# LSTM gates as seven half-size products for two groups at a time, and layer 2's output through DRAM

## The chip, the cores and the metric

The kernel runs on one core of a Trainium2 chip. The metric is the device time of one execution in microseconds (us), taken as the median of several runs. TensorE (PE) multiplies matrices into PSUM; VectorE (DVE), ScalarE (ACT) and GpSimd (POOL) do the elementwise work; SyncE (SP) issues the DMAs.

## What is computed

Four graph layers, each followed by a residual sum and a layernorm, on x of 128 batches x 64 nodes x 256 features, all in float32. The first three are a graph attention, an attention over 512 edges, and a graph convolution with a two-layer network and batch norm. The fourth is the one that the change is about: two graph convolutions, then LSTMs of 256 hidden units over windows of 1, 2, 3 and 4 nodes, one after the other, each of which writes its last output back into h.

```python
def step(carry, x_t):
    h, c = carry
    g = x_t @ Wih.T + h @ Whh.T + bias
    i, f, gg, o = jnp.split(g, 4, axis=-1)
    c = jax.nn.sigmoid(f) * c + jax.nn.sigmoid(i) * jnp.tanh(gg)
    h = jax.nn.sigmoid(o) * jnp.tanh(c)
    return ((h, c), None)
...
h = jax.nn.relu(jnp.einsum('ts,bsh->bth', adj, x @ Wg0 + bg0))
h = jax.nn.relu(jnp.einsum('ts,bsh->bth', adj, h @ Wg1 + bg1))
for p in range(1, MAX_SKIP + 1):
    nw = Tv // p
    wins = h[:, :nw * p, :].reshape(Bv * nw, p, Hd)
    last = _lstm_last(Wih[p - 1], Whh[p - 1], bih[p - 1], bhh[p - 1], wins)
    idx = jnp.arange(nw) * p + (p - 1)
    h = h.at[:, idx, :].set(last.reshape(Bv, nw, Hd))
```

## The kernel before

The 128 batches are worked in 16 blocks of 512 tokens (`q`) in layers 0 to 2. Layer 2's result stays in SBUF in the tile `A`, 1024 float32 in each of 128 partitions for each block (`leave`, L791). Layer 3 takes it in eight groups of 16 batches (`g`), each of two halves (a half is one block).

`gcn(g, half, ...)` is layer 3 for a half, cut in pieces by `yield`: the batch norm's scale on ACT (L890), a transpose (on TensorE for group 0 at L897, through DVE and a round trip over DRAM, `turned`, for the later ones), the residual sum and layernorm (`norm`; bn_stats on DVE at L92, a power on GpSimd at L83, the scaling on GpSimd at L97), the products with the adjacency (`neighbours`, L878) and with Wg0 and Wg1 (L933, L945), and the write of `H` (L956 on DVE, L957 on ACT).

`lstm(g)` runs the windows p = 1 to 4 on one group. The hidden size of 256 is two halves of 128 (`j` for outputs, `k` for inputs). A unit of work is one half j of one step: for each of the gates i, f, g, o, two matmuls with `wih` (L994) and, after the first step, two with `whh` (L1000) accumulate in one of five PSUM banks, over 512 columns for p=1 and p=2, 336 for p=3 and 256 for p=4. ACT takes each bank through sigmoid or tanh (L1006); DVE and GpSimd form the cell (L1009 to L1011, or L1013 in the first step); ACT its tanh (L1014); DVE the output (L1021, L1023). A float32 matmul in the program is two instructions in the profile.

After every unit, pieces of the next group's `gcn` and of `final` (the last residual sum, layernorm and store of a group, for one of four node residues s) are put in by a written list of units (`AT`, `side`). They are ordered behind the last instruction on ACT, DVE and GpSimd. SP issues nearly all loads and stores in program order. The weights of all four p are loaded once: `wih` and `whh` of 1 MB each for p=2, 3, 4.

The prologue of layer 3 runs the two halves of group 0 in turn before the first LSTM unit, and the last `final` (with `pieces=2`) follows the last unit.

Of the kernel before, what the change touches and what calls it, by code (L numbers as in the profile page):

```python
# [41 lines left out]
def kernel(ctx: ExitStack, tc: tile.TileContext, i, out):  # L42
# [9 lines left out]
    A = main.tile([P, NQ, 2 * QT], F32, name="A")  # L52
# [32 lines left out]
    def layernorm(dst, src, n, engine):  # L85

        st = small.tile([P, n, 6], F32, name="ln_st", bufs=6)
        mv = small.tile([P, n, 2], F32, name="ln_mv", bufs=6)
        both = small.tile([P, 2, n], F32, name="ln_rs", bufs=6)
        rs, ng = both[:, 0, :], both[:, 1, :]  # L90
        for r in range(n):
            nc.vector.bn_stats(st[:, r, :], src[:, r, :])  # L92
            nc.vector.bn_aggr(mv[:, r, :], st[:, r, :])
        rsqrt(rs, mv[:, :, 1], n)
        nc.vector.tensor_scalar_mul(ng, mv[:, :, 0], -1.0)  # L95
        for r in range(n):
            engine.tensor_scalar(dst[:, r, :], src[:, r, :], ng[:, r:r + 1], rs[:, r:r + 1],  # L97
                                 op0=OP.add, op1=OP.mult)
# [13 lines left out]
    with ExitStack() as two:  # L112
        wa = two.enter_context(tc.tile_pool(name="wa", bufs=1))
# [12 lines left out]
        def load_x(q):  # L126
            xin[q] = xp.tile([P, PQ, D], F32, name="xin")
            nc.sync.dma_start(xin[q], x_view[q])
            if q:

                rows = i["x"][q * QT:(q + 1) * QT, :].rearrange("(j t) (k i f) -> i k t j f", t=32, k=KD, f=32)
                for n in range(4):
                    for k in range(KD):
                        to = A[n * 32:(n + 1) * 32, q, k * QT:(k + 1) * QT]
                        nc.sync.dma_start(to.rearrange("t (j f) -> t j f", f=32), rows[n, k])

        class su:

            free = NQ * 2 * QT

            @classmethod
            def tile(cls, shape, dtype, name):
# [4 lines left out]
                t = A.rearrange("p q c -> p (q c)")[:shape[0], cls.free:cls.free + size]  # L147
# [60 lines left out]
        def token_major(q):  # L208

            return A[:, q, :].rearrange("p (c d) -> p c d", c=PQ)  # L210

# [3 lines left out]
        def l0_a(q):  # L215
            L0[q] = {"x": xin.pop(q)}
            if q:

                L0[q]["xT"] = work.tile([P, KD, QT], F32, name="tT", bufs=1)
                nc.vector.transpose(L0[q]["xT"].rearrange("p k t -> p (k t)"), A[:, q, :])  # L220
# [199 lines left out]
        def v_c(q, one=True):  # L420
# [14 lines left out]
            dst = A[:, q, :].rearrange("p (b s n) -> p s b n", b=KD * PQ, s=2)  # L435
# [270 lines left out]
        def hidden(q, m):  # L706
            return Z[q][:, m, :] if m < 2 else A[:, q, (m - 2) * QT:(m - 1) * QT]

# [7 lines left out]
        def up(q, m):  # L716
            p_ = pbank()
            for k in range(KD):
                nc.tensor.matmul(p_, w1[:, k, m * P:(m + 1) * P], A[:, q, k * QT:(k + 1) * QT],  # L719
# [31 lines left out]
        wih, whh = {}, {}  # L751
        wih[1] = wd.tile([P, KD, 3 * D], F32, name="wih1")
        v1 = i["WihT"][0].rearrange("(k p) c -> p k c", p=P)
        nc.sync.dma_start(wih[1][:, :, :D], v1[:, :, :D])
        nc.sync.dma_start(wih[1][:, :, D:], v1[:, :, 2 * D:])
        wih[2] = weights(wd, "wih2", i["WihT"][1])
        whh[2] = weights(wd, "whh2", i["WhhT"][1])
# [30 lines left out]
        def leave(q, m, p_):  # L788

            dst = A[:, q, :].rearrange("p (n m t) -> p n m t", n=PQ, m=M2)[:, :, m, :]  # L790
            nc.vector.tensor_scalar_add(dst, p_.rearrange("p (n t) -> p n t", n=PQ), b2[:, m:m + 1])  # L791

# [33 lines left out]
    work = ctx.enter_context(tc.tile_pool(name="work3", bufs=2, reuse_waits="tile"))  # L826
    ps = ctx.enter_context(tc.tile_pool(name="ps3", bufs=1, space=PSUM, reuse_waits="tile"))
    for p in (3, 4):
        wih[p] = weights(we, f"wih{p}", i["WihT"][p - 1])
        whh[p] = weights(we, f"whh{p}", i["WhhT"][p - 1])  # L830
    out_view = out.rearrange("(b t) d -> b t d", t=N)
    HT = QT // 2
    GB = 16
    ST = 5
    TC = P // GB
    NG = NB // GB
    assert GB * N == 2 * QT

    def gbank(shape):
        return ps.tile([P] + shape, F32, name="g", bufs=3)  # L840

    def lbank(shape):
        return ps.tile([P] + shape, F32, name="l", bufs=5)


    rb = we.tile([P, KD, P], F32, name="rb")
# [7 lines left out]
    Hs, lasts = {}, {}  # L854
# [27 lines left out]
    def gcn(g, half, bank, name):  # L882

        q = g * 2 + half
        def fetch(a):
            x = work.tile([P, 2, D], F32, name="x2r", bufs=4)
            nc.sync.dma_start(x.rearrange("p c d -> p (c d)"), x2_dram[q][:, a * 2 * D:(a + 1) * 2 * D])
            z = A[:, q, a * QT:(a + 1) * QT].rearrange("p (c m t) -> p c m t", c=2, m=KD)
# [3 lines left out]
            if g:  # L892
                return x, turned(z.rearrange("p c m t -> p (c m) t"))
# [4 lines left out]
            return x, xt  # L898

        def norm(a, x, xt):  # L900
            xv = x.rearrange("p c (m i f) -> p c m i f", m=KD, f=32) if g else x
            nc.vector.tensor_add(xv, xt, xv)
            x3 = A[:, q, a * QT:(a + 1) * QT].rearrange("p (c d) -> p c d", c=2)
# [5 lines left out]
        if g:  # L909
# [4 lines left out]
            for a in range(2):  # L914
                norm(a, *came[a])
                yield
        else:
            for a in range(2):
                norm(a, *fetch(a))
                yield  # L920

        x3 = A[:, q, :].rearrange("p (c d) -> p c d", c=PQ)
        p_ = neighbours(bank, lambda c, f: x3[:, c, f:f + 64])
        hT = work.tile([P, KD, QT], F32, name=name, bufs=2)
# [4 lines left out]
        hN = work.tile([P, KD, QT], F32, name=name, bufs=2)  # L929
# [23 lines left out]
        if g not in Hs:  # L953
            Hs[g] = work.tile([P, KD, N, GB], F32, name="H")
        dst = Hs[g].rearrange("p k t (h c s) -> p h s k c t", h=2, s=2)[:, half]
# [4 lines left out]
    GCN_STEPS = 8  # L960

    def lstm(g):

        H = Hs[g]
        for p in range(1, SKIP + 1):
            nw = N // p
            nww = min(nw, QT // GB)
            for w0 in range(0, nw, nww):

                Hw = H[:, :, w0 * p:(w0 + nww) * p, :].rearrange("p k (w s) b -> p k w s b", s=p)  # L970
                cell = work.tile([P, KD, nww, GB], F32, name="cell", bufs=1)
                hid = None
                for s in range(p):
                    last = s == p - 1

                    over = last and p < SKIP
                    if over:
                        new = None
                    elif last:

                        new = work.tile([P, 2, KD, P], F32, name="hd", bufs=3)
                    else:
                        new = work.tile([P, KD, nww, GB], F32, name="hid")
                    ends = []
                    for j in range(KD):
                        gates = {}
                        names = ("i", "f", "g", "o") if s else ("i", "g", "o")
                        for n in names:
                            gates[n] = ps.tile([P, nww, GB], F32, name="l", bufs=5)
                        for n in names:  # L990
                            m = 2 * "ifgo".index(n) + j
                            mw = m - 2 if p == 1 and m > 1 else m
                            for k in range(KD):
                                nc.tensor.matmul(gates[n], wih[p][:, k, mw * P:(mw + 1) * P], Hw[:, k, :, s, :],  # L994
                                                 start=k == 0, stop=not s and k == KD - 1)
                        if s:
                            for n in names:
                                m = 2 * "ifgo".index(n) + j
                                for k in range(KD):
                                    nc.tensor.matmul(gates[n], whh[p][:, k, m * P:(m + 1) * P], hid[:, k],  # L1000
                                                     start=False, stop=k == KD - 1)
                        act = {}
# [135 lines left out]
```

## Time and profile before

| | us |
|---|---|
| median of 3 runs (2138.45 to 2139.91) | 2138.93 |
| the profiled execution | 2138.25 |
| its span, first to last instruction | 2136.4 |
| end of layer 2's last matmuls | 771.5 |
| first LSTM matmul | 807.4 |
| last LSTM matmul | 2126 |

The granted TensorE clock was 0.987 on average. HBM traffic was 67.45 MB read and 44.04 MB written, at a mean DMA load of 53 GB/s. In the profile, a group's "busy" is the time that its instructions cover together, its "mean" the duration of one from issue to end; matmuls overlap, so the mean is longer than the distance between two of them. "Idle before" is the time that the engine stood still ahead of the group, with the engine and line that ended most of it. In rows in order of time, the first number is the start, the second the time covered, and xN says how many instructions are merged.

### The profile page before, as it was taken

How to read it: one execution, taken by the hardware profiler on the slowest of the kernel's cores; microseconds unless marked ns; L12 is line 12 of the kernel's file. 1: busy time of each engine (PE TensorE's matmuls, PEld its weight loads, DVE VectorE, ACT ScalarE, POOL GpSimd, SP SyncE). 2: the span in 40 equal slices, each digit the busy share in tenths (PEclk: the TensorE clock that was granted, in tenths of full speed). 3: DMA queues.
4: the chain of work that ended last, by engine and by line, in shares of the span. 5: the costliest groups of instructions: out<-in, count | busy, mean ns of one | idle time of the engine just before them, and what ended most of it. 6: DMA issues, size and time to landing. Idle time of an engine off the chain costs nothing.

```text
span 2136.4 us, 29441 instructions
## 1 busy us (share of the span) xinstructions
PE 2060.7 (96%) x11343; PEld 1330.1 (62%) x11343; DVE 885.9 (41%) x2069; ACT 932.1 (44%) x1795; POOL 430.1 (20%) x569
## 2 busy tenths in 40 slices
PE   5999999998999989999999999999999999999998
PEld 4666767665544444585576576577467468468467
DVE  7456566654444343333234334324324324323213
ACT  2776666664339014334234334334334334333333
POOL 1134334332210010121112112113103103102012
PEclk8999999998999989999999999999999999999999
DMA  5244532322240021012112102103103102101001
GB/s 144 63 69 73 85 61 53 52 43 43 43 118 29 0 89 60 21 54 66 40 46 74 40 29 90 40 11 99 50 6 104 50 1 89 50 1 60 20 1 60
DMA packets 232636, 113.41 MB, mean 53 GB/s; under 512 B 150192, under 2 KB 215728, under 8 KB 232240
## 3 DMA queue, kind: packets, MB, share of 16 engines
q1 hardware_dynamic: 230640, 109.57, 20.2%
q8 instruction: 89, 1.46, 0.3%
q0 software_dynamic: 1024, 1.05, 0.2%
q10 hardware_dynamic: 832, 0.92, 0.1%
q14 instruction: 51, 0.42, 0.1%
HBM read 67.45 MB, written 44.04 MB: 52 GB/s over the span
## 4 chain that ended last, share of the span: by engine, by line
PE 86%; DVE 6%; ACT 4%; issue 2%; POOL 1%; DMA 1%; SPq 0%; POOLq 0%; DVEq 0%; ACTq 0%
PE l L994 36%; PE l L1000 20%; PE pz L784 5%; PE pz L719 5%; PE e L323 3%; PE g L933 2%; PE g L945 2%; PE m L295 2%; PE m L230 2%; PE z L332 2%; PE m L298 2%; PE g L878 1%; PE m L413 1%; PE m L270 1%; ACT u L334 1%
## 5 line engine op out<-in xcount | busy, mean ns | idle before, releaser
L994 PE MATMUL l<-H,wih 128*128 128x256 f32 (+2 forms) x2496 | 787.5, 470 | 1.8 <-ACT H L957 1.2
L994 PEld LDWEIGHTS l<-H,wih 128*128 128x128 f32 x2496 | 471.4, 190 | 286.2 <-issue 185.6
L1000 PE MATMUL l<-hid,whh 128*128 128x256 f32 (+2 forms) x1536 | 435.9, 437 | 0.0
L1000 PEld LDWEIGHTS l<-hid,whh 128*128 128x128 f32 x1536 | 291.8, 190 | 128.4 <-issue 61.2
L1006 ACT ACTIVATE gate_i<-l,bias 128x256 f32<-128x256 f32 (+2 forms) x176 | 100.3, 570 | 441.9 <-PE l L1000 374.2
L1010 POOL TENSOR_TENSOR cell<-gate_f,cell 128x256 f32<-128x256 f32 (+2 forms) x96 | 85.0, 885 | 726.0 <-ACT gate_f L1006 726.0
L1009 DVE TENSOR_TENSOR gate_i<-gate_i,gate_g 128x256 f32<-128x256 f32 (+2 forms) x96 | 49.6, 517 | 415.1 <-ACT gate_g L1006 415.0
L83 POOL TENSOR_TENSOR ln_rs<-ln_rs,mhalf 128x2 f32<-128x2 f32 (+2 forms) x97 | 82.0, 846 | 571.6 <-DVE ln_rs L95 570.7
L334 ACT ACTIVATE u<-z 128x1024 f32<-128x1024 f32 x128 | 130.3, 1025 | 63.3 <-PE z L332 62.3
L1006 ACT ACTIVATE gate_g<-l,bias 128x256 f32<-128x256 f32 (+2 forms) x176 | 100.3, 570 | 107.9 <-PE l L994 59.5
L1014 ACT ACTIVATE gate_g<-cell 128x256 f32<-128x256 f32 (+2 forms) x176 | 90.0, 511 | 86.9 <-DVE cell L1013 45.0
L1013 DVE TENSOR_TENSOR cell<-gate_i,gate_g 128x512 f32<-128x512 f32 (+2 forms) x80 | 48.2, 602 | 186.5 <-ACT gate_g L1006 186.4
L1006 ACT ACTIVATE gate_o<-l,bias 128x256 f32<-128x256 f32 (+2 forms) x176 | 99.3, 564 | 59.9 <-PE l L1000 54.0
L719 PE MATMUL pz<-A,w 128*128 128x512 f32 x256 | 113.1, 595 | 0.0
L332 PE MATMUL z<-gath_r,qs 128*128 128x512 f32 x256 | 100.4, 480 | 0.7 <-ACT u L334 0.4
L306 DVE TENSOR_TENSOR qs<-m,qs 64x256 fp32r<-64x256 f32 x128 | 54.0, 422 | 107.0 <-ACT qs L305 104.8
L719 PEld LDWEIGHTS pz<-A,w 128*128 128x128 f32 x256 | 47.9, 190 | 55.3 <-issue 53.3
L295 PE MATMUL m<-wq,tT 128*128 128x260 f32 x256 | 71.8, 403 | 7.8 <-ACT yT L403 5.4
L1006 ACT ACTIVATE gate_f<-l,bias 128x256 f32<-128x256 f32 (+2 forms) x96 | 51.1, 532 | 59.6 <-PE l L1000 59.1
L1023 DVE TENSOR_TENSOR hid<-gate_o,gate_g 128x256 f32<-128x256 f32 (+2 forms) x96 | 47.4, 493 | 61.2 <-ACT gate_o L1006 35.1
L721 DVE BATCH_NORM_STATS2 st<-pz 128x6 f32<-128x512 f32 x64 | 44.4, 697 | 59.5 <-PE pz L719 59.4
L1023 DVE TENSOR_TENSOR H<-gate_o,gate_g 128x512 f32<-128x512 f32 (+1 forms) x64 | 41.3, 645 | 66.6 <-PE l L994 46.1
(242 smaller groups left out, 2525.2 us busy)
## 6 DMA issues: line engine op xcount, KB each, us to landing
way<-st SPq DMA_DIRECT2D x59, 256.0 KB
st<-way SPq DMA_DIRECT2D x236, 64.0 KB
xin<-in_x SPq DMA_DIRECT2D x16, 512.0 KB
ld<-table SPq DMA_DIRECT2D x16, 512.0 KB
x_dram<-y SPq DMA_DIRECT2D x16, 512.0 KB
x2r<-x_dram SPq DMA_DIRECT2D x32, 256.0 KB
x_dram<-A SPq DMA_DIRECT2D x64, 128.0 KB
x3r<-x_dram SPq DMA_DIRECT2D x64, 128.0 KB
```

Source lines behind the costliest of these rows:

```text
L83: nc.gpsimd.tensor_tensor(dst, dst, mhalf[:, :n], OP.pow)
L295: nc.tensor.matmul(pq, xT[:, k, c * P:(c + 1) * P], wq[:, k, :], start=k == 0, stop=k == KD - 1)
L332: nc.tensor.matmul(z[:, k, :], L1[q]["qs"][c][:, s, k * P:(k + 1) * P], gath_r, start=True, stop=True)
L334: nc.scalar.activation(u, z, AF.Relu)
L719: nc.tensor.matmul(p_, w1[:, k, m * P:(m + 1) * P], A[:, q, k * QT:(k + 1) * QT], start=k == 0, stop=k == KD - 1)
L784: nc.tensor.matmul(p_, w2[:, k, m * P:(m + 1) * P], hidden(q, k), start=k == 0, stop=k == M1 - 1)
L994: nc.tensor.matmul(gates[n], wih[p][:, k, mw * P:(mw + 1) * P], Hw[:, k, :, s, :], start=k == 0, stop=not s and k == KD - 1)
L1000: nc.tensor.matmul(gates[n], whh[p][:, k, m * P:(m + 1) * P], hid[:, k], start=False, stop=k == KD - 1)
L1006: nc.scalar.activation(act[n], gates[n], AF.Tanh if n == "g" else AF.Sigmoid, bias=bias[:, p - 1, m:m + 1])
L1010: nc.gpsimd.tensor_tensor(cell[:, j], act["f"], cell[:, j], OP.mult)
L1014: nc.scalar.activation(act["g"], cell[:, j], AF.Tanh)
L1023: nc.vector.tensor_mul(Hw[:, jj, :, s, :] if over else new[:, jj], o, t)
```

## The change

Three things change.

1. **Two groups at a time, seven products.** `lstm(pair)` treats two groups (n = 0, 1) together. In every step after the first of p = 2 to 4, a gate's 2 x 2 blocks of weights (output half, input half) times the 2 x 2 blocks of inputs (input half, group) are formed with seven products of 128 x 128 blocks instead of eight, for the input with `wih` and for the hidden state with `whh`, both accumulated in one bank. For this the sums of weight blocks (`Weights.sums`, four GpSimd adds for each source), of input blocks (`input_sums`, four GpSimd adds a step) and of hidden blocks (`hidden_sums`, two on DVE and two on GpSimd) are formed beforehand, and the seven products are put together by two ACT copies, five DVE adds and two GpSimd adds a gate (`Gate.use`). The gates run one after the other, f, g, i, o. Each gate's activations, cell work and tanh are issued within the next gate (`prev.act`, `prev.after`, `prev.tanh`). At a step's end the first four products' input parts of the next step's gate f are issued ahead of the outputs (`nxt.part`). p=2 runs in two runs of 16 windows, so that its matmuls have 256 columns. First steps (`plain`) keep their plain products, at 256 columns for p=2.
2. **An order for all engines.** `given` issues every piece behind the latest instruction of each of PE, DVE, ACT and GpSimd. Pieces of `gcn`, `final` and the weights' `prepare` go to written units of a pair (48 of them, of kinds "at", "gap" and "wait").
3. **Layer 2's output through DRAM.** `A` is split: blocks 0 to 3 stay in `A0`; blocks 4 to 15 are written to `z_dram` as they are done, and are read back into `A0` by `gcn`. The space gives room to weights with their sums; the weights of p = 2, 3 and 4 are loaded anew for each pair, into two alternating buffers. Halves 2 and 3 are transposed on TensorE too, and the prologue runs parts of four halves. The PSUM banks go from five "l" and three "g" to six and two.

```diff
-    A = main.tile([P, NQ, 2 * QT], F32, name="A")
+    A0 = main.tile([P, NA, 2 * QT], F32, name="A0")
+    z_dram = [dram.tile([P, 2 * QT], F32, name=f"z_dram{q}") for q in range(NQ)]
...
+            if q >= NA and m == M2 - 1:
+                nc.sync.dma_start(z_dram[q], Aq(q))
...
+            for dst, a, b, op in ((S3, a11, a21, sub), (S1, a21, a22, add), (S2, S1, a11, sub), (S4, a12, S2, sub)):
+                nc.gpsimd.tensor_tensor(dst, a, b, op)
...
+            def sums_of(dst, b11, b12, b21, b22, fast, slow, between=None):
+                fast.tensor_tensor(dst[:, 0], b12, b11, OP.subtract)
+                if between:
+                    between()
+                fast.tensor_tensor(dst[:, 1], b22, dst[:, 0], OP.subtract)
+                slow.tensor_tensor(dst[:, 2], b22, b12, OP.subtract)
+                slow.tensor_tensor(dst[:, 3], b21, dst[:, 1], OP.subtract)
...
+                def product(self, j):
+                    for src in range(2):
+                        given(self.part, j, src)
+                    given(self.use, j)
+
+                def use(self, j):
+                    b, k, t = self.banks[j], self.kept, self.t
+                    if j in (1, 5):
+                        nc.scalar.activation(self.keep(j), b, AF.Copy)
+                    elif j == 2:
+                        nc.vector.tensor_add(t[0][:, 0], b, k[1])
+                    elif j == 6:
+                        nc.vector.tensor_add(t[0][:, 1], b, k[1])
+                    elif j == 7:
+                        nc.vector.tensor_add(self.keep(7), b, t[0][:, 1])
+                        nc.gpsimd.tensor_tensor(t[1][:, 1], k[7], k[5], OP.add)
+                        nc.gpsimd.tensor_tensor(t[0][:, 1], t[0][:, 1], k[5], OP.add)
+                    elif j == 4:
+                        nc.vector.tensor_add(t[1][:, 0], b, k[7])
+                    else:
+                        nc.vector.tensor_add(t[0][:, 1], b, t[0][:, 1])
...
+                        names = "fgio"
+                        for at, n in enumerate(names):
+                            G = nxt or Gate(n, r, s, tiles)
+                            nxt = None
+                            G.product(1)
+                            G.product(5)
+                            if prev:
+                                prev.act(1)
+                                prev.act(0)
+                                prev.after(1)
+                            G.product(2)
+                            if prev:
+                                prev.after(0)
+                                prev.tanh(1)
+                            G.product(6)
+                            if n == "o":
+                                G.act(0, 0)
+                            if prev:
+                                prev.tanh(0)
+                            G.product(7)
+                            if at == 1:
+                                given(input_sums, r, s + 1)
+                            if at < 3:
+                                G.product(4)
+                                G.product(3)
+                                yield "at", unit
...
+                        o.product(4)
+                        given(output, r, s, 0, o.tiles["o"], o.tiles["g"], (0,))
+                        o.act(1)
+                        o.product(3)
+                        o.act(0, 1)
+                    if not last:
+                        tiles = {}
+                        nxt = Gate("f", r, s + 1, tiles)
+                        for j in (1, 5, 2, 6):
+                            given(nxt.part, j, 0)
+                    elif p < SKIP:
+                        yield "wait", unit + 1
+                    if s:
+                        given(output, r, s, 0, o.tiles["o"], o.tiles["g"], (1,))
+                        given(hidden_sums, s, lambda: output(r, s, 1, o.tiles["o"], o.tiles["g"], (0, 1)))
...
+                put(k + 1, final(g, SKIP - 1), n, n + 2)
+        if k < NP - 1:
+            put(k, prepare(weights_of[k + 1, 2]), 34, 41, 43)
+            for n, keys in enumerate([
+                    [0, 2, 3, 5, 6, 10, 15, 17, WAIT(22), GAP(22), 24],
+                    [2, 5, 6, 8, 9, 19, GAP(25), 26, GAP(29), 30, 32],
+                    [6, 8, 9, 12, 13, 27, WAIT(33), GAP(33), GAP(36), 37, 39],
+                    [9, 11, 12, 15, 16, 38, GAP(40), 41, GAP(44), 45, 47]]):
+                put(k, gcn((k + 1) * 2 + n // 2, n % 2, gbank, "hT"), *keys)
```

In a pair, units 0 to 7 are p=1, 8 to 21 p=2, 22 to 32 p=3 and 33 to 47 p=4; within p=4, step 0 is units 33 to 35, and then each step has a unit after f, g and i and one at its end.

## The prediction

> **What bounds the kernel now.** I read the page first (busy shares, slices, chain), then the busy time of three stretches, then TensorE's groups by shape, then single steps in order of time. The page:
>
> ```profile
> PE 2060.7 (96%) x11343; PEld 1330.1 (62%) x11343; DVE 885.9 (41%) x2069; ACT 932.1 (44%) x1795; POOL 430.1 (20%) x569
> ...
> PE   5999999998999989999999999999999999999998
> ...
> PE 86%; DVE 6%; ACT 4%; issue 2%; POOL 1%; DMA 1%; SPq 0%; POOLq 0%; DVEq 0%; ACTq 0%
> ```
>
> TensorE is the only engine near its span, and the chain that ended last runs on it. The stretches (columns: PE, PEld, DVE, ACT, POOL busy, clock, DMA) show the start of layer 3, its LSTM and the tail:
>
> ```profile
> 771.50:807.40 35.90, 26.53 (x323) 19.12 (x322) 19.61 (x51) 7.76 (x12) 7.62 (x13) 0.76 0.40 133
> 807.40:2126.00 1318.60, 1317.36 (x6160) 856.05 (x6161) 443.61 (x1002) 499.09 (x911) 226.51 (x321) 1.00 0.15 47
> 2126.00:2137.00 11.00, 0.95 (x6) 0.41 (x4) 3.14 (x13) 0.89 (x2) 2.19 (x4) 0.67 0.09 24
> ```
>
> In the LSTM, TensorE idles 1.2 us of 1318.6. A matmul taken out there is worth its full pitch, and a microsecond of new waiting costs a microsecond. The matmuls by shape:
>
> ```profile
> L994 PE MATMUL l<-H,wih 128*128 128x512 f32 x832 | 363.6, 593 | 1.8 <-ACT H L957 1.2 <-ACT gate_g L1014 0.5
> L994 PE MATMUL l<-H,wih 128*128 128x256 f32 x960 | 217.2, 380 | 0.0
> L994 PE MATMUL l<-H,wih 128*128 128x336 f32 x704 | 206.8, 448 | 0.0
> L1000 PE MATMUL l<-hid,whh 128*128 128x256 f32 x768 | 173.6, 379 | 0.0
> L1000 PE MATMUL l<-hid,whh 128*128 128x336 f32 x512 | 149.9, 446 | 0.0
> L1000 PE MATMUL l<-hid,whh 128*128 128x512 f32 x256 | 112.5, 592 | 0.0
> ```
>
> The mean is a latency; the pitch is what counts. Starts in order of time: 16 of 256 columns take 3.455 us (1949.51 to 1952.96), 16 of 336 take 4.52, 16 of 512 take 6.866. So 0.216, 0.2825 and 0.429 us for each instruction, and each product in the program is two of them. The pitch is linear in columns, so halving a matmul's width costs nothing.
>
> **What the Trainium skill says.** "TensorE: Matmul & The Clock Gate", Part 1: after an idle window of about 3.4 us the array runs at half clock until about 3.4 us of work have passed. The trace agrees; the first four products after the gaps at the start took twice the time of the next:
>
> ```profile
> 788.66 3.43 PE L933 MATMUL g<-hT,wg 128*128 128x512 f32 x4
> ...
> 791.93 1.88 PE L933 MATMUL l<-hid,wg 128*128 128x512 f32 x4
> ```
>
> "SBUF — State Buffer", Who interferes with whom: a VectorE instruction with two SBUF inputs and a GpSimd instruction that reads SBUF exclude each other; one with a single SBUF input is free. The trace has mild cases, 0.58 instead of 0.42 us:
>
> ```profile
> 2107.51 0.72 POOL L1010 TENSOR_TENSOR cell<-gate_f,cell 128x256 f32<-128x256 f32 x1
> 2108.18 0.94 POOL L1035 COPY hd<-H 128x256 f32<-128x256 f32 x2
> 2108.27 0.58 DVE L1011 TENSOR_TENSOR cell<-cell,gate_i 128x256 f32<-128x256 f32 x1 [2.48 <-POOL cell L1010]
> ...
> 2121.97 0.42 DVE L1011 TENSOR_TENSOR cell<-cell,gate_i 128x256 f32<-128x256 f32 x1 [2.48 <-POOL cell L1010]
> ```
>
> **The change part by part.**
>
> *Matmuls.* Later steps go from 8 to 7 products for each gate, source and pair. p=2: 512 instructions of 512 columns (219.7 us) become 4 pairs x 2 runs x 4 gates x 7 x 2 sources x 2 = 896 of 256 (193.5): -26.2. p=3: 1024 to 896 of 336: -36.2. p=4: 1536 to 1344 of 256: -41.5. p=2's first step, 192 of 512 to 384 of 256: +0.5. Sum -103.4. Halves 2 and 3 are now transposed on TensorE: 16 more at about 0.21 (0.85 for four at L897): +3.4.
>
> Each still hides its weight load, 0.19 under 0.216 (PEld rows of a step: 3.43 for 16 beside 3.62).
>
> *The additions beside them.* A p=4 product with both sources takes 0.86 us, a gate 6.05. A gate adds two ACT copies (0.39, L232's 258-column row), five VectorE adds (0.43) and two GpSimd adds (0.72). At 2.2 us of DVE in 6.05 they are hidden in gates f, g and i. PSUM has six banks, so TensorE may run 5 us ahead. Not so in gate o, where i's finish also lies. From o's start U: ACT copies product 5 at 1.9 to 2.3, then i's two sigmoids (0.63 each) to 3.55; DVE mul and add for m=1 (0.69 each) 2.95 to 4.33, use of product 2 to 4.76, m=0's mul and add to 6.14, uses of 6 and 7 to 7.0; GpSimd's two adds to 8.5; DVE's use of product 3 to 8.96; ACT to 9.48; hid to 9.93; first hidden sum 10.35. TensorE finishes o at 6.05, runs four prefetched products and one more part (5 x 0.432) to 8.21 and then wants that sum. It waits 2.2 us, and 0.25 for the second half of hid: 2.45. The same chain with p=3 (DVE 0.51 and 0.86, GpSimd 0.89, product 1.13): 2.25. At the end of p=2 and p=3 the next p wants hid almost at once: 4.05 and 4.7.
>
> *Fillers.* In pairs 0 to 2 a layer-3 product (1.72 us) is put at each of these boundaries, two at each change of p. What is left: 2 x 0.75 + 0.5 + 0.6 + 1.2 = 3.8, three times 11.4. Pair 3 has no next groups: 2 x 2.45 + 2.25 + 4.05 + 4.7 = 15.9.
>
> Behind a waiting part of product 5 stand, in TensorE's order, all products of the next gate f, and behind those f's copies on ACT and adds on DVE; nothing else can use the time, since the order is written out.
>
> *GpSimd.* Weight sums are 4 x 1.27 us a half (L1010's 512 row). At unit 9 they stand, after 3.2 us of input sums, ahead of the hidden sums of p=2's first step; these end 1.7 us late, some 2.4 where a norm is added and a neighbour product fills: 9 us over four pairs. Elsewhere (27, 28, 41, 43) GpSimd has slack. Two final steps and a transpose on DVE at units 38 and 42 exceed the 2.4 us in which DVE waits for ACT: about 0.6 each, 5 in all.
>
> *DRAM.* Twelve writes and reads of z (0.5 MB), and 12 more loads of 1 MB. Before, five landings (1 MB and four of 256 KB) took 5.7 us at 772; three z reads and six weight loads in a pair's 310 us are little. On SP the last z write stands ahead of x2r, instead of a weight load: +1. Loads come units before their use: 0, and 20 if I am wrong on that.
>
> *The start.* Before the first LSTM product TensorE now waits for half 3's second norm: DVE 2.1 and GpSimd 1.8, some 4 us more idle than now. With x2r +5. Group 1's input is written right before its use: +1.3 (H write 1.06).
>
> *At nothing.* Layer 3's products keep two banks instead of three: DVE takes one within 0.9 us of its end (L935, 0.69), and the next comes a unit (5 us) later; if the cover is gone, 0.9 for each. Five layernorm buffers for six, and layer 2's split tile: no instruction changes there. The first step's gates in joined banks: ACT does one 512-wide instruction (0.69) for two of 256 (0.47 each), off the path.
>
> *The tail.* Two groups' last layernorms follow the last product. Two more pieces of 0.9 on DVE, and the last hid 2.1 later than now: +4.
>
> *Clock.* Idle of 4 us at the start and at pair 3's two changes of p may each bring 1.7 us at half clock: +5, from 0 to 8.
>
> Sum: -103.4 + 3.4 + 11.4 + 15.9 + 9 + 5 + 5 + 1.3 + 4 + 5 = -43.4. On the profiled span of 2136.4 that is 2093.0; that execution took 2138.25, 1.85 more, so 2094.9. The median of the runs is 0.7 above it: 2095.
>
> The bounds: the waits (41 us) lie between 0 and about 70, if contention on the shared port adds half a microsecond to each of the nine two-input DVE instructions in the critical part of seven steps; the rest gives 10 either way.
>
> **The rivals.**
> - *All waits covered*: shorter chains or more fill than I count, no cold clock. -103.4 + 3.4 + 5 + 1.3 + 4 = -89.7: 2049. For it: 41% and 44% of DVE and ACT. Against: an average hides what gate o packs together. Chance 0.2.
> - *A transfer blocks SP*: a weight load's wait for its buffer holds up x2r, z or the final's rows, and ACT or DVE, in order, wait for them. For it: all DMAs are on SP, and DVE already waits 68.4 us in all at L1049 for st. Against: final's parts are now two units (12 us) apart. Some 20 us more: 2115. Chance 0.06.
> - *Slower: the shared port*. A later step has about 16 GpSimd instructions that read SBUF (13 us of 24) and 9 two-input DVE ones in its recurrent part. If each DVE one waits half a GpSimd instruction (0.36) and the GpSimd ones in turn push the keeps and banks, a step loses over 3 us in all 28 steps and not only where pair 3 is bare: +84, 2179. It decides from 43.4 / 28 = 1.55 us a step. For it: 0.58 against 0.42 with only 20% of GpSimd. Against: the five uses read PSUM and have one SBUF input. Chance 0.12.
>
> **How the numbers follow.** My sum has 0.62, with its own range of 2072 to 2120. Down to 2048 most of the first rival comes in, up to 2125 the second; what is left out is the port and the edges, near 0.2. A measurement here can tell about 0.2% (4 us). Faster 0.86, within 0.02, slower 0.12.
>
> **What would show it.** TensorE's matmuls rise from 11343 by 256 in the LSTM (3264 become 3520, narrower ones) and 20 transposes to about 11619, and its busy time falls to about 1961. Idle is to appear as waits of the matmuls on hid or hsums for DVE, 2 to 5 us each, nearly all in pair 3, and on half 3's norm at the start. GpSimd doubles to over 800 us, DVE passes 1100. If TensorE has waits inside gates f, g and i, or on banks held by a use, my picture of six banks is wrong; if the idle of the LSTM is under 10 us, the first rival holds; if L1011's kin average over 0.6 us at 256 columns, the third.

## The result and the profile after

The changed kernel takes **2163.82 us** (median of 4 runs, 2158.48 to 2167.28); the kernel before took 2138.69 (2138.09 to 2139.91) beside it. The ratio is 1.0115, with a 95% interval of 1.0093 to 1.0136: slower, where 2095 was forecast. The profiled execution took 2164.74 us, with a span of 2163.0.

The page of the changed kernel: busy shares, TensorE's and its clock's slices, shares of the chain that ended last.

```profile
PE 2006.5 (93%) x11619; PEld 1398.3 (65%) x11619; DVE 1158.6 (54%) x2563; ACT 957.2 (44%) x1807; POOL 860.1 (40%) x1018
...
PE   5999999998999988999998999998999999999896
...
PEclk8999999999999989999999999999999999999998
...
PE 62%; DVE 17%; POOL 10%; ACT 5%; issue 3%; DMA 1%; SPq 0%; DVEq 0%; POOLq 0%; ACTq 0%
```

The instruction count is the forecast one, and DVE and GpSimd are as busy as was said. But TensorE is busy for 2006.5 us, where 1961 was forecast, and it now holds 62% of the chain instead of 86%: DVE's and GpSimd's work stands in it with 27%. The same three stretches as before (the start of layer 3, its LSTM, the tail; columns PE, PEld, DVE, ACT, POOL, clock, DMA share, GB/s):

```profile
772.00:820.50 48.50, 34.00 (x467) 24.78 (x466) 28.27 (x80) 13.67 (x24) 15.56 (x26) 0.78 0.72 243
820.50:2147.20 1326.70, 1254.42 (x6292) 918.28 (x6288) 703.50 (x1451) 518.73 (x913) 644.81 (x752) 0.97 0.19 62
2147.20:2163.00 15.80, 2.44 (x9) 1.17 (x8) 7.44 (x29) 1.86 (x3) 5.91 (x10) 0.61 0.24 67
```

In the LSTM TensorE stands still for over 70 us where it stood still for 1.2, and its mean clock is 0.97 instead of 1.00. TensorE's waits, from the view of waits (what was waited for; us in total, times, longest):

```profile
PE g L1004 <- ACT H L1028: 12.7, 9, 1.8
PE l L1196 <- DVE hs L1090: 11.6, 6, 2.8
PE l L1196 <- DVE hid L1123: 9.4, 3, 3.2
PE l L1196 <- DVE gate L1213: 8.7, 6, 2.1
...
PE l L1196 <- DVE gate L1215: 6.2, 5, 1.2
```

L1090 is the step's own chain at its boundary, which was foreseen; the three waits for L1123 are the first boundary of a run of two, shown below. L1213 and L1215 are waits of a gate's product for a bank that DVE has not yet read, inside a step; the forecast named these as the sign that its picture of six banks is wrong. The first row is a piece of layer 3's next group, put there to fill a boundary, that waits itself.

To see where the time went, I split the time from each matmul's start to the next one's into three: the distance that this shape usually has, the waiting before the next one, and the remainder (half clock, and what else a product takes longer). Over the whole span:

```
                  usual distance   waiting   remainder
before                 1958.6        62.0      101.8
after                  1857.5       141.7      148.5
difference             -101.1       +79.7      +46.7    = +25.3, and 1.3 after the last matmul
```

The 100 us of the seven-product scheme (Strassen's, as it is called below) came in full. The waits took 80 of them back, and the remainder another 47.

**The half clock.** In the clock records the LSTM of before has no slice under full speed; the changed one has 14 stretches at 0.50, of 3.4 or 6.8 us, which cost 28.4 us of work (busy time in them, times one half). In order of time at a boundary of p=3 in the last pair (start, time covered, xN instructions; 2 of 336 columns take 0.565 us at full clock):

```profile
2009.54 0.83 PE L1196 MATMUL l<-hid,wh 128*128 128x336 f32 x2 [0.51 <-DVE hid L1126]
2013.18 0.83 PE L1196 MATMUL l<-hs,wh 128*128 128x336 f32 x2 [2.81 <-DVE hs L1090]
2013.85 1.07 PE L1196 MATMUL l<-hid,wh 128*128 128x336 f32 x2
2014.72 1.32 PE L1196 MATMUL l<-hs,wh 128*128 128x336 f32 x2
2015.84 1.32 PE L1196 MATMUL l<-xs,wx 128*128 128x336 f32 x2
2016.96 1.01 PE L1196 MATMUL l<-hs,wh 128*128 128x336 f32 x2
2017.80 0.73 PE L1196 MATMUL l<-xs,wx 128*128 128x336 f32 x2
2018.37 0.73 PE L1196 MATMUL l<-hs,wh 128*128 128x336 f32 x2
```

From 2014.72 to 2015.84 a pair takes 1.12 us, twice its usual time, and from 2017.80 on 0.57 again. The wait of 2.81 us was followed by 1.7 us more.

**Two places that return in three pairs.** At the first boundary of a run of two, GpSimd, DVE and TensorE:

```profile
1561.47 5.96 POOL L895 TENSOR_TENSOR wx<-wx 128x512 f32<-128x512 f32 x4
...
1563.17 1.27 DVE L98 TENSOR_SCALAR ln_rs<-ln_mv 128x2 f32<-128x2 f32 x1
1564.36 0.70 DVE L922 STREAM_TRANSPOSE st<-A 128x512 f32<-128x512 f32 x1
1564.98 2.99 DVE L1123 TENSOR_TENSOR hid<-gate 128x512 f32<-128x512 f32 x2
...
1568.03 1.22 PE L1196 MATMUL l<-hid,wh 128*128 128x256 f32 x2 [3.08 <-DVE hid L1123]
```

While GpSimd adds weights (unit 9), two DVE products that take 1.25 us together in the rows of experiment 8 below take 2.99, and TensorE waits for the second. At units 41 and 42:

```profile
1800.29 5.20 POOL L895 TENSOR_TENSOR wx<-wx 128x512 f32<-128x512 f32 x4
1805.44 0.73 POOL L1218 TENSOR_TENSOR gate<-kept 128x256 f32<-128x256 f32 x1
...
1806.88 0.42 DVE L1223 TENSOR_TENSOR gate<-l,gate 128x256 f32<-128x256 f32 x1 [5.06 <-POOL gate L1219]
1807.56 0.71 DVE L922 STREAM_TRANSPOSE st<-hd 128x512 f32<-128x512 f32 x1 [0.26 <-POOL hd L1313]
...
1811.93 0.67 PE L1196 MATMUL l<-xs,wx 128*128 128x256 f32 x2 [2.14 <-DVE gate L1213]
1813.84 1.22 PE L1196 MATMUL l<-H,wx 128*128 128x256 f32 x2 [1.24 <-DVE gate L1215]
```

The same block of weight sums stands on GpSimd ahead of gate i's two adds. DVE, in order, waits 5.06 us for them; the final's transpose and layernorm, which stand next on DVE, then stand ahead of i's cell and gate o's first use (L1213), and TensorE runs out of banks.

### The profile page after: what moved, and what is told of

Read it like the earlier page. It is cut to its first block, busy times and chain, and to the rows that moved or that the text cites. A ratio compares the mean times of both kernels' runs of the same rounds, so it can differ in the third digit from the quotient of the medians.

```text
span 2163.0 us, 31461 instructions
## 1 busy us (share of the span) xinstructions
PE 2006.5 (93%) x11619; PEld 1398.3 (65%) x11619; DVE 1158.6 (54%) x2563; ACT 957.2 (44%) x1807; POOL 860.1 (40%) x1018
## 4 chain that ended last, share of the span: by engine, by line
PE 62%; DVE 17%; POOL 10%; ACT 5%; issue 3%; DMA 1%; SPq 0%; DVEq 0%; POOLq 0%; ACTq 0%
PE l L1196 20%; PE l L1053 8%; PE l L1161 6%; PE pz L789 5%; PE pz L727 5%; PE e L331 2%; PE m L303 2%; PE g L1004 2%; POOL gate L1219 2%; DVE cell L1140 2%; DVE ln_st L95 2%; POOL gate L1218 2%; PE m L306 2%; DVE gate L1139 2%; PE z L340 2%
## 5 line engine op out<-in xcount | busy, mean ns | idle before, releaser
L1196 PE MATMUL l<-xs,wx 128*128 128x256 f32 (+1 forms) x896 | 289.2, 405 | 16.6 <-DVE gate L1213 8.7
L1196 PE MATMUL l<-hs,wh 128*128 128x256 f32 (+1 forms) x896 | 290.2, 406 | 11.6 <-DVE hs L1090 11.6
L1196 PE MATMUL l<-hid,wh 128*128 128x256 f32 (+1 forms) x672 | 217.6, 406 | 10.7 <-DVE hid L1123 9.4
L1196 PE MATMUL l<-H,wx 128*128 128x256 f32 (+1 forms) x672 | 215.7, 403 | 6.3 <-DVE gate L1215 6.2
L1196 PEld LDWEIGHTS l<-xs,wx 128*128 128x128 f32 x896 | 170.6, 193 | 65.8 <-POOL ln_rs L86 7.5
L1196 PEld LDWEIGHTS l<-hs,wh 128*128 128x128 f32 x896 | 172.2, 194 | 57.2 <-DVE hs L1090 15.5
L1228 ACT ACTIVATE gate<-gate,bias 128x512 f32<-128x512 f32 (+3 forms) x252 | 170.6, 702 | 73.2 <-POOL gate L1218 44.5
L1161 PE MATMUL l<-H,wx 128*128 128x256 f32 (+1 forms) x768 | 189.0, 406 | 9.2 <-DVE H L1126 5.1
L1161 PEld LDWEIGHTS l<-H,wx 128*128 128x128 f32 x768 | 149.7, 196 | 51.4 <-issue 7.0
L1053 PE MATMUL l<-H,wih 128*128 128x512 f32 x384 | 167.7, 597 | 1.7 <-DVE H L1027 1.7
L1196 PEld LDWEIGHTS l<-H,wx 128*128 128x128 f32 x672 | 126.9, 191 | 40.0 <-DVE gate L1215 8.8
L1053 PEld LDWEIGHTS l<-H,wih 128*128 128x128 f32 x384 | 73.0, 191 | 91.8 <-issue 85.1
L1223 DVE TENSOR_TENSOR gate<-l,gate 128x256 f32<-128x256 f32 (+1 forms) x112 | 50.2, 449 | 148.9 <-POOL gate L1219 148.9
```

Source lines behind the costliest of these rows:

```text
L1053: nc.tensor.matmul(b, wih1[:, k, mw * P:(mw + 1) * P], Hw[:, k], start=k == 0, stop=k == KD - 1)
L1161: nc.tensor.matmul(one, w.raw[0][:, k, at, m, :], inp(r, 0, k)[:, g], start=k == 0, stop=k == KD - 1)
L1196: nc.tensor.matmul(self.banks[j], lhs, rhs, start=src == 0, stop=src == 1)
L1228: given(lambda: nc.scalar.activation(dst, dst, f, bias=b))
```

## The experiments

My theory after the traces: three things cost the gain, namely the weight sums' place on GpSimd, layer 3's pieces with two banks, and the half clock behind the waits. The rivals: the waits are the step's own chain and only change their name; or the new structure (pairs, a given order, the detour through DRAM) is dear by itself. Medians of each run, and my split from the first product of the LSTM to the first one behind its last:

```
                      us    waiting  half clock  usual distance
before            2138.7       1.2       0.0        1293.1
after             2163.8      74.5      28.4        1189.0
e1_fill           2161.5      42.7      14.7        1230.0
e2_sums           2143.8      64.7      15.3        1189.0
e3_order          2150.7      66.3      24.7        1189.0
e4_eight          2175.0      15.9       3.4        1294.3
e5_both           2116.1      49.0       9.0        1189.0
e6_bothfill       2115.1      28.3       3.3        1215.7
e7_start          2110.0      29.1       4.9        1216.2
e8_norm           2114.1      50.2      10.2        1189.4
e9_unit9          2159.6      69.8      27.9        1189.0
e10_unit41        2149.1      61.4      25.5        1189.0
```

(Before: 2138.0 to 2140.2 in the three groups of runs of the experiments. Waiting and half clock are of the one profiled execution. 2.2 us of each waiting, but 0.2 in 4 and none in before, lie behind the LSTM's last product.)

**1. Repeats in the waits.** At a boundary the first product is issued again, as a finished product of its own, into the same bank; in the last pair also where p changes:

```diff
+            def again(G, j, count):
+                for _ in range(count):
+                    G.part(j, 0, True)
...
                         for j in (1, 5, 2, 6):
+                            if j == 1 and early + soon:
+                                given(again, nxt, 1, max(early, 1))
+                                continue
```

> Repeats, where TensorE would stand still between two steps, a product that it has just issued (in the first three pairs 7 at the first boundary of a run of two, 3 at the second run's, 2 at either boundary of a run of three, 4 at one of a run of four; in the last pair 5 at the later boundaries and a few at a change of p). About 90 products of 0.43 to 0.86 us more in all, and nothing else. Theory CLOCK (the waits of 1 to 3 us cost their length and, soon after, 3.4 or 6.8 us at half the clock): the half-clock windows next to the filled waits go, some 15 to 25 of the 28.5 us that they cost in this stage, and the repeats cost only what they overshoot the waits: 2143, from 2135 to 2152. Rival IDLE (the waits themselves are the loss and the half-clock windows have another cause): windows stay, overshoot comes on top: 2163 or more.

Measured: 2161.5 (ratio to before 1.0105, 1.0088 to 1.0122). The half-clock stretches fell from 14 to 6, their loss from 28.4 to 14.7 us; all those behind the last pair's own boundaries went. But the repeats added 41 us of products and took only 32 of waiting: I had put in too many. The clock follows the waits, as the theory says; the time does not show it, and the forecast of 2143 missed (2135 to 2152).

**2. Weight sums elsewhere.**

```diff
-            put(k, prepare(weights_of[k, 3]), 0, 9, 11)
+            put(k, prepare(weights_of[k, 3]), 0, 4, 6)
...
-            put(k, prepare(weights_of[k + 1, 2]), 34, 41, 43)
+            part = prepare(weights_of[k + 1, 2])
+            put(k, part, 34)
+            put(k + 1, part, 1, 3)
```

> GpSimd's eight sums of weight halves for each set of weights are placed in units of plain steps (units 5 and 6 or 4 and 6 for three steps, 1 and 3 of the next pair for two) in place of units 9, 11, 41 and 43. Theory GPSIMD (they hold the port that VectorE needs at unit 9, and gate i's own GpSimd sums at unit 41): the wait of 3.1 us at the first boundary of the run of two and those of 0.8, 2.1 and 1.2 us in gate g at units 41 to 42 go, in three pairs each, with the half-clock windows behind them: 21 us of waits and 8 to 15 of half clock less, about 2135 (2128 to 2148). Rival (other GpSimd work, norms and input sums, would do the same there): under 8 us, 2156 to 2164.

Measured: 2143.8, 20 us less. The place at unit 41 is clear. At the start of the runs of two the waits for the inputs' sums on GpSimd grew from 3.6 to 12.0 us, the longest of them 5.3. To part the two, each half of the edit ran alone.

> The changed kernel with the sums of the weights for three steps alone moved, from units 9 and 11 to units 4 and 6 (5 and 6 in the first pair). Theory PORT (at unit 9 they slow VectorE's product for the hidden state from 0.7 to 1.5 us): the waits of 3.1 us go: 3 times 3.1, and 3 half-clock slices of 1.5 to 2.9: 2148 (2144 to 2156). Rival QUEUE (a block of 6 us on GpSimd costs a wait of that size wherever a normalization or a sum of inputs stands behind it, in units 4 and 6 too): 2158 to 2166.

Measured: 2159.6, only 4.2 less, with an interval (1.0086 to 1.0120) that overlaps the changed kernel's: the rival holds. What stands there now, in the kernel with only unit 9's sums moved:

```profile
1202.73 6.15 POOL L895 TENSOR_TENSOR wh<-wh 128x512 f32<-128x512 f32 x4
1208.84 1.15 POOL L86 TENSOR_TENSOR ln_rs<-ln_rs,mhalf 128x2 f32<-128x2 f32 x1
...
1214.55 0.69 DVE L972 TENSOR_TENSOR x2r<-st,x2r 128x512 f32<-128x512 f32 x1 [5.12 <-DMA st<-way]
...
1216.53 0.70 POOL L86 TENSOR_TENSOR ln_rs<-ln_rs,mhalf 128x2 f32<-128x2 f32 x1 [5.35 <-DVE ln_rs L98]
...
1218.63 0.73 POOL L1090 TENSOR_TENSOR xs<-H 128x256 f32<-128x256 f32 x1
...
1219.42 0.70 PE L1196 MATMUL l<-xs,wx 128*128 128x256 f32 x2 [2.28 <-POOL xs L1090]
```

The block now delays a normalization. SP, in program order, stores that one's result before it brings back the rows that the next normalization needs; DVE waits 5.12 us for them, and the inputs' sums, behind the next normalization in GpSimd's queue, come late with it. The waits for L1123 (9.4 us) are gone, as the theory said; others came in their place. At either place six microseconds in one piece were paid by what stood behind them.

> The changed kernel with the sums of the next pair's weights alone moved, from units 41 and 43 to units 1 and 3 of that pair. Theory (at unit 41 they put off gate i's GpSimd sums, and gate i's end then stands behind the final's work on VectorE): waits of 0.8, 2.1 and 1.2 us and those after unit 43 of 0.4 and 0.9 go, and 4 to 6 us of half clock: 3 times 5.5 and 5: 2143 (2138 to 2150). Rival (the final's work on VectorE delays the gate there by itself): 2156 or more.

Measured: 2149.1, 14.7 less; the waits for L1213 (8.7 us) are gone from the table of waits. Theory right in kind, forecast 6 us too good: a new wait of 1.2 us for L1090 stands at the step's end there, in three pairs, and the half clock fell by 2.9 us where 4 to 6 were forecast. The two halves together, 4.2 and 14.7, make the 20 of the joint edit within what runs vary.

**3. Pieces of layer 3 a unit earlier.** The forecast had put the two banks at nothing. In time order, the last piece of one half (L940), its reading by ACT, and the next half's piece in the gap:

```profile
1108.77 1.16 PE L940 MATMUL g<-bdT,st 64*64 64x64 f32 x64
...
1110.68 1.03 ACT L1028 ACTIVATE H<-g 128x512 f32<-128x512 f32 x1
...
1111.76 1.98 PE L1004 MATMUL g<-hT,wg 128*128 128x512 f32 x4 [1.84 <-ACT H L1028]
```

The one stands right ahead of the other, and the bank is read only 1.8 us after its last product. In three of the four lists:

```diff
-                    [0, 2, 3, 5, 6, 10, 15, 17, WAIT(22), GAP(22), 24],
+                    [0, 2, 3, 5, 6, 10, 15, 17, WAIT(22), GAP(22), 23],
```

(and 30, 32 to 30, 31; and 37, 39 to 36, 37).

> The last pieces of the half finals come a unit earlier (unit 23 for 24, 31 for 32, 36 and 37 for 37 and 39), so that their bank is read before the pieces of the next group that come in the gaps. Theory BANKS (with two banks in place of three a piece in the gap waits until the final's last sum has read the older): the waits of layer 3's product for H, 1.2 to 1.8 us each, 12.7 us in all, mostly go, with part of the half clock behind them: 2148 (2140 to 2156). Rival (the banks only pass the wait on: the piece then waits for its own operands, or the gap is shorter and the next product waits instead): 2160 to 2166.

Measured: 2150.7, 13 less. The waits of L1004 for H are gone from the waits, and some came back as waits for L1090 (11.6 to 15.3 us) and L1123 (H: 4.1 to 8.1), since a boundary that was covered by a waiting piece is now covered by a short one. Theory right; over the whole span the waiting fell by 8 us, the remainder by 8.

**4. Eight plain products in the same structure.** Each gate computes its eight products; the sums of weights, inputs, hidden states and products are not there.

```diff
+                        for k in range(KD):
+                            rhs = hid[:, k, g] if src else inp(self.r, self.s, k)[:, g]
+                            nc.tensor.matmul(one, w.raw[src][:, k, self.at, m, :], rhs,
...
-                        rhs = (hsums if src else xsums[r, s])[:, (3, 0, 1, 2)[j - 4]]
-                    nc.tensor.matmul(self.banks[j], lhs, rhs, start=src == 0, stop=src == 1)
```

> Keeps the pairs of groups, the order given by hand, layer 2's output through DRAM and the reloaded weights, and computes each gate as eight plain products again: no sums of weights, inputs or hidden states, and no sums of products. Theory WAITS (Strassen's arithmetic gains its 100 us of TensorE and loses as much to waits and half clock): TensorE's matmul time returns by 100 us, waits of the stage fall from 74 to under 15 us, hardly any half-clock window is left in it: 2150 (2135 to 2165), that is about what the changed kernel takes. Rival STRUCTURE (pairs, order and the DRAM detour themselves cost 50 us or more): 2190 and above, with waits of 40 us and more left.

Measured: 2175.0 (ratio 1.0157, 1.0140 to 1.0174), between the two forecasts. TensorE's table of waits of this kernel has for the LSTM

```profile
PE g L1003 <- ACT H L1027: 11.1, 9, 1.3
...
PE l L1160 <- DVE H L1122: 2.8, 2, 1.5
```

and nothing longer but one of 1.7 at the first step: the waits inside steps are Strassen's, those of the two banks are the structure's. So the structure alone costs some 35 us against the before of its own group of runs (2140.2; 38.4 between the profiled spans). Of that the first LSTM product, at 823.1 instead of 807.4, is 15.7 (pieces of the third and fourth half group stand ahead of it, which earlier lay in the LSTM), the LSTM 20.2 (14.7 of waiting), the tail the rest. Strassen on top of it took 105 us off the products and 11 off the time.

**5. Both orders.** The sums go one add at a time, at most three in a unit, and a run's input sums come a unit earlier:

```diff
                 nc.gpsimd.tensor_tensor(dst, a, b, op)
+                yield
...
-            put(k, prepare(weights_of[k, 3]), 0, 9, 11)
+            put(k, prepare(weights_of[k, 3]), 0, 4, 4, 4, 5, 6, 7, 7, 7)
...
-            put(k, prepare(weights_of[k, 4]), 23, 27, 28)
+            put(k, prepare(weights_of[k, 4]), 23, 24, 24, 25, 26, 27, 29, 30, 31)
...
+            put(k + 1, part, 0, 0, 1, 1, 2, 2, 3, 3)
...
-                            if at == 1:
+                            if at == 0:
                                 given(input_sums, r, 1)
```

and experiment 3's lists.

> Both edits of the order together, the sums of weights now one at a time (one to three in a unit of layer 3's first step, one in a unit of the third set) and the sums of a run's inputs a unit earlier. Theory (waits and half clock are separate places that add up; the 5.3 us wait that the block of sums opened at the start of the runs of two goes too): idle of the stage 76 to about 50 us, half clock and drain 65 to about 47, so 2119 (2108 to 2130). Rival (the places take each other's gain: what is mended at one boundary comes late at the next): 2131 or more.

Measured: **2116.1** (ratio to before 0.9906, 0.9890 to 0.9923), as forecast. Nothing was taken out of the computation; 48 us came from the order alone. That is some 15 more than 2 and 3 gave together, with the single adds and the earlier input sums, which were not tried apart; the waits of 12.0 us for those sums are gone. What leads the table of waits now is the steps' chain and, where p changes, the last outputs, which the next p reads:

```profile
PE l L1196 <- DVE hs L1090: 17.7, 12, 2.7
PE l L1161 <- DVE H L1123: 8.0, 7, 2.1
PE l L1196 <- DVE hid L1123: 7.3, 3, 2.5
```

**6. The same with repeats**, fewer than in 1.

> The same with repeated products only where no other work is left to fill a wait (last pair; later boundaries of the runs of three and four). Theory CLOCK: about 14 half-clock windows of 1.4 to 3 us each less 4 to 8 us of overshoot: 2107, some 10 to 14 below the same without repeats. Rival IDLE (clock follows something else than these waits): the same or a few us above.

Measured: 2115.1, no difference; the forecast of 2107 missed. Half-clock stretches fell from 4 to 2 (9.0 to 3.3 us), waiting by 21 us, and the repeats took 27. So the clock does follow the waits, but idle work did not sell that here: the repeats took 6 us more than the waiting that they filled, which is what the clock gave back.

**7. The fourth half group's last piece behind the first unit**, on top of 6:

> The same again, with the last aggregation of the fourth half group taken out of the prologue and done after layer 3's first unit, so that the first unit doesn't stand behind it. Theory: layer 3's first product at 814 in place of 820: 2101, 5 to 7 less. Rival (the piece's operands are late wherever it is put, and layer 3 then waits for it at unit 4): no change within 2 us.

Measured: **2110.0** (2108.4 to 2116.1; ratio to before 0.9872, 0.9855 to 0.9888), the lowest of all. The forecast of 2101 missed; against 6 it is 5 us less, as was said, but the traces do not show these 5 at the start. The first product of the LSTM came at 818.4, not at 814 (820.0 in 6), in a profiled execution that was itself the slowest of the four. In experiment 8, with the same edit, it came at 816.8 against 817.6 in 5. What the start gives is not settled.

**8. A normalization moved off a boundary**, 5 with 7's start, without repeats (in the fourth list the load and what follows it come one or two units later as well):

```diff
-                    [2, 5, 6, 8, 9, 19, GAP(25), 26, GAP(29), 30, 31],
+                    [2, 5, 6, 8, 11, 19, GAP(25), 26, GAP(29), 30, 31],
```

> The kernel with both edits of the order and the earlier start, without repeats, and with the second normalization of the second half group moved from unit 9, where VectorE does it ahead of the product that makes the new hidden state, to unit 11 (the fourth half group's load with it). Theory: the waits of 2.5 us at the first boundary of the run of two, and the half-clock slice behind, go in three pairs (3 times 1.3 to 4): 2104 (2098 to 2110). Rival (the step's own chain from the last product through ScalarE to VectorE is as long): 2110 or more.

Measured: 2114.1; the rival's time, for a reason that neither had. In this kernel, in order of time:

```profile
1204.70 1.43 DVE L972 TENSOR_TENSOR x2r<-st,x2r 128x512 f32<-128x512 f32 x1 [2.93 <-DMA st<-way]
...
1208.06 0.64 DVE L1142 TENSOR_TENSOR cell<-gate 128x512 f32<-128x512 f32 x1
...
1211.23 1.08 ACT L959 ACTIVATE A<-A,sh,sc 128x256 f32<-128x256 f32 x2
1212.21 1.24 ACT L1166 ACTIVATE gate<-l,bias 128x512 f32<-128x512 f32 x2
...
1213.05 1.25 DVE L1123 TENSOR_TENSOR hid<-gate 128x512 f32<-128x512 f32 x2
...
1214.35 0.70 PE L1196 MATMUL l<-hid,wh 128*128 128x256 f32 x2 [2.51 <-DVE hid L1123]
```

The normalization of unit 8, late by its own DMA, and unit 9's scaling on ACT (L959) stand ahead of gate i's cell and gate o's sigmoid. In the last pair, where no such work is put in, the same boundary has no wait at all. Of the two normalizations in units 8 and 9 I had moved the second; the first was not tried.

## Why the prediction was wrong

Its terms against what the two traces show:

- **Matmuls and transposes**, -103.4 + 3.4: measured -101.1, with the 11619 instructions that were named. Right.
- **The last pair's boundaries**, 15.9: 18.4. **The start**, +5: 2.4 more of waiting within 772 to 820.5, some 3 more ahead of it, and 5 more of slow array. **The tail**, +4: 16.0 instead of 10.5, so 5.5. Near, but for the 5 of slow array, which belong to the clock.
- **The other three pairs**, 11.4 + 9 + 5 + 1.3 = 26.7: LSTM waits are 72.3 in all, so about 54 here beside 1.2 before. This is the first failed step. Two of its sentences failed, and a third had its size by luck:
  - "Elsewhere (27, 28, 41, 43) GpSimd has slack." It had slack in busy time, but not at that moment. Moving 41 and 43 alone gave 14.7 us. The step looked at who waits for the sums of weights, not at who stands behind them: gate i's adds, then DVE, then the banks.
  - "At nothing: Layer 3's products keep two banks instead of three." The bound of 0.9 for each had DVE reading a bank within 0.9 us of its end, and the next piece a unit (5 us) later. But the written list has one half's last piece right ahead of the gap in which the next half's piece stands, ACT was done with the bank 1.8 us after its last product, and nine fillers waited 1.2 to 1.8 us. Moving pieces gave 13 us.
  - Unit 9's sums were priced at 9 us for four pairs, by their length in GpSimd's queue ahead of the hidden sums. The waits there are 9.4 us in three pairs, near that by luck: TensorE waits for DVE's product, and DVE is what is held, 2.99 us for two products. Moving the sums bought only 4 us, since they delay others elsewhere.
- **Clock**, "+5, from 0 to 8", from waits of about 4 us only. The second failed step, and with what goes beside it the larger; its root is the sentence that "a microsecond of new waiting costs a microsecond". The remainder rose by 46.7 us: 28.4 is half clock in the LSTM, 5 the start. Of the other 13, some 9 stand at the waits themselves: at each of the 55 in the LSTM the next instruction starts 0.18 us later than wait and usual distance together, since one of 256 columns lasts 0.38 us, where the next usually starts 0.216 behind its start. The last 4 stay open.

  The section of "TensorE: Matmul & The Clock Gate" (Trainium skill, Part 1) on which the step rested speaks of an idle window of about 3.4 us; here waits of 1.9 to 3.2 us in all were enough, and the measurement decides. The trace of before has such a case, which the forecast passed over when it wrote "The trace agrees": its longest stretch at half clock begins at 774.48, behind 3.41 us in which TensorE stood still for 2.2, in two waits (same columns as above).

```profile
771.07:774.48 3.41, 1.18 (x6) 0.42 (x4) 2.66 (x5) 0.00 (x0) 0.05 (x1) 1.00 0.49 129
774.48:777.89 3.41, 2.08 (x10) 2.09 (x10) 1.65 (x7) 2.08 (x4) 0.49 (x1) 0.51 1.00 392
```

- **The rivals.** The shared port, at 2179, was nearest in time, and is at most a part of what happened. DVE's products of two SBUF inputs did take longer:

```profile
L1140 DVE TENSOR_TENSOR cell<-cell,gate 128x512 f32<-128x512 f32 x40 | 31.3, 783 | 1.4
L1093 DVE TENSOR_TENSOR hs<-hid,hs 128x336 f32<-128x336 f32 x8 | 8.7, 1094 | 0.3
```

  In before, 512 columns took 692 ns and 336 took 508. My estimate, from the durations over the usual one of each width, is 40 us of DVE's time in the LSTM, 9 of them beside the 512-wide weight sums; the rival has 28 x 9 x 0.36 = 91. Its sign, L1011's kin at 0.6 instead of 0.42, stays away: L1140 is 13% longer, not 43%, and the five uses, which the forecast took to be free of it, stay at 0.42 us for 256 columns (L1213 to L1223, medians). How much of the 40 us reached TensorE was not measured apart from unit 9. The loss sits at a few places, not in all 28 steps. Transfers did not hold DVE in the changed kernel: its waits for `st` on its way back from DRAM fell from 68.4 to 2.1 us, and no wait of SP for a buffer showed in the chain (DMA 1%).

The outcome by the largest term: a wait was priced at its length. In the LSTM the 71 us of new waits came with 41 more. And a third of the waits was the order's, not the arithmetic's: with the order mended, 49 us of waiting and 9 of half clock remain, and the same arithmetic is 1% faster than before instead of 1% slower. Against eight products in the same structure, in its unmended order, that is 59 of 105 us; eight products in the mended order were not run, so what the arithmetic alone gives there is open.

## What to carry to other kernels

When an engine's slack is used for more work, cut the work into pieces no longer than the slack at each place, and ask for each piece who is queued behind it in the next few microseconds; busy shares of 20 or 40% said nothing on this here. A filler only fills if its own bank and operands are free, so follow it back one step further. And a kernel at full TensorE has one more price for new waits, the clock, where they add up within a few microseconds: to spread short waits rather than let two fall together follows from the counts below, and was not tried.

## What the hardware showed

The half-clock stretches of a run all begin on one grid: their starts differ by whole multiples of 3.413 us over the whole run, and nearly all last one or two such slices. I took all full-clock slices of the LSTM in five runs (after, 2, 3, 5, 6) and added up the waiting in each. All 35 with 1.89 us or more were followed by a slice at half clock; of the 108 with 0.8 to 1.85 us, five were; of the 1702 with less, none. Four of those five also held 1.1 to 2.1 us of 64 x 64 products (L940), the fifth came a slice after a half-clock one. In the other six runs (1, 4, 7 to 10) it is 27 of 28 with 1.88 us or more, 12 of 108, and none of 2103. So a wait of 1.7 us alone cost its length (at 860.4 in the changed kernel), and two waits that only together reached 1.9 us in a slice cost 1.4 to 3.1 more. Where a wait falls on the grid is luck, which may be part of why the changed kernel's runs spread over 9 us and those of before over 2; that was not tested.
